# First layer of a four-layer graph network: a fixed TensorE order from the third column on, with one product ahead of the diagonal's sums

## The chip, the cores and the metric

One core of a Trainium2 chip. The metric is device time in microseconds (us); 25 timed runs of the kernel before in the last session have a median of 2253.3 us and lie between 2250.0 and 2257.1. Columns and blocks are counted from 0, so "column 2" is the third column.

## The reference, cut to what matters

Four layers pass `x` (4096 x 128) through a dense-stored 4096 x 4096 adjacency `adj`, each with a residual and a layer normalization. Only the first is changed:

```python
hw = h @ W
pos = (node_adj > 0).astype(hw.dtype)
...
h_plus = pos @ hw
e_plus = leaky_relu((h_plus @ a1 + h_minus @ a2)[:, 0], ALPHA)
scores = where(edge_adj > 0, e_plus[None, :], NEG_INF)      # cut
attn = softmax(scores, axis=1)
h_prime = attn * edge_adj @ hw
```

The score of an edge depends on its column alone. So, with weights `xe = exp(e)`, the softmax is a product of the adjacency with `xe * hw`, divided by a product of its mask with `xe`. The catch is that `e` of a column of 512 nodes needs the whole column of masks first.

## The kernel before

The adjacency is cut into 8 x 8 blocks of 512 x 512 (1 MB each). For column i the kernel reads block (i, j), VectorE makes the mask `pos`, TensorE adds up *edge sums* of the mask (short matmuls, four at a time in 32-column strips: four take 0.40 us in the trace, against 1.04 us for four over all 128 columns) and, for the blocks whose scores are already known (j < i), a *product* of the block with the scaled `hw` (four fp32 matmuls of 128 x 512, 3.4 us). When the edge sums of column i are whole, the scores of its nodes can be made:

```python
def scores(i, pe):
    parts <- pe                                   # VectorE or ScalarE
    sums = columns(parts)                         # TensorE: "score columns"
    e, den, leaky, clip on VectorE; exp on ScalarE
    nc.vector.tensor_mul(hw[:, tb, :], hw[:, tb, :], xe...)
    split3(xp[:, tb, :], 3, xe[:, tb])            # xp: three bf16 parts of xe
```

Only then can the blocks that waited for these scores be done: the diagonal's (i, i), and the two blocks above it that were kept in SBUF, (i-2, i) and (i-1, i), so that they are not read again. Their sums need `xp`, their products only `hw`. Blocks further above are read again in a *second sweep*. From column 3 on TensorE's order is pinned by `in_order`; the order of the other engines is the scheduler's.

```python
for i in range(3, NB):
    ...
    for g, group in enumerate(groups):            # two blocks a group
        got = [sums_of(i, j, ...) for j in group] # cut
        if g == 1:
            diagonal_sums(*rest)                  # needs xp
            for k in (i - 3, i - 2):
                above_sums(k, i - 1, kept[k, i - 1])
            diagonal_product(*rest)
        for n, (j, a, pos) in enumerate(got):
            if j < i:
                product(p, j, a, j == 0, False)
            if g == 0 and n == 0 and waiting:
                scores(i - 1, rest[2])
            if g == 1 and n < 2:
                above_product(i - 3 + n, i - 1, kept.pop(...))
```

TensorE's results go to PSUM, which this kernel divides into four pools of two banks: `ps_acc` (products), `ps_den` (edge sums), `ps_mm` (sums of kept blocks) and `ps_tr` (transposes and score columns). Blocks come into five rotating buffers.

## Time and profile before

| | before |
|---|---|
| median of the first three runs | 2254.38 us |
| span of the profiled run | 2250.1 us |
| TensorE busy | 95% |
| mean granted TensorE clock | 0.986 |
| first layer, to its last transposes | about 350 us |

In the timelines quoted below a line gives the start (us from the span's start), the length, engine, line of the source, operation, output<-inputs and shape, and in brackets the idle time before it with the instruction that ended it. `pden<-pos,xp` are the sums that wait for xp, `pacc<-chunk,hw` a product, `pacc<-keep,hw` a product of a kept block, `ptr<-sel,parts` the score columns. PE is TensorE, DVE VectorE, ACT ScalarE; L379 is line 379 of the kernel; `numT` is where the products of all columns are added up. A product's four fp32 matmuls show as x8 in these lines. A half-clock window is a stretch in which the trace shows a granted clock of 0.50, as from 82 to 88 us in before. The prediction shows the lines of before.

### The profile page before, as it was taken

To read this page: it belongs to the slowest core of one execution; us is meant where nothing else is said; L and a number is where in the kernel's file an instruction comes from. 1 tells how busy PE (TensorE), PEld (TensorE's weight loads), DVE (VectorE), ACT (ScalarE), POOL (GpSimd) and SP (SyncE) were. 2 spreads that over 40 slices of the span, in tenths; PEclk is the share of its full clock that TensorE was granted. 3 is DMA by queue.
4 is the path that set the end of the run, shared out by engine and by line. 5 is a ranking of instruction groups with operands and counts; after the bars stand their busy time and mean duration, and the time that the engine had idled before them with its cause. 6 is when DMAs were issued, how large, how long until landed. Compare 5 with 4: busy or idle time off the path is not lost. (4 is left out here: it accounts for less than half of the span.)

```text
span 2250.1 us, 22965 instructions
## 1 busy us (share of the span) xinstructions
PE 2140.8 (95%) x8633; PEld 847.8 (38%) x8636; DVE 1184.4 (53%) x1832; ACT 563.4 (25%) x1014; POOL 857.3 (38%) x539
## 2 busy tenths in 40 slices
PE   8899999999999999999999999978999899999997
PEld 3334354444444444444443333322222222233333
DVE  5544472000011100000025777789999999999995
ACT  6645110000000000000032322335333433332213
POOL 0000000000000000000004666688999899989990
PEclk9999999999999999999999999989999999999999
DMA  9776658888777676778766556614666566645544
GB/s 393 300 270 245 219 185 274 302 299 300 263 257 244 227 271 236 264 270 279 264 237 229 206 206 219 220 67 169 240 228 231 200 241 246 219 139 204 187 169 170
DMA packets 87145, 528.18 MB, mean 235 GB/s; under 512 B 9328, under 2 KB 15472, under 8 KB 25712
## 3 DMA queue, kind: packets, MB, share of 16 engines
q1 hardware_dynamic: 80288, 521.64, 65.7%
q10 hardware_dynamic: 6736, 4.98, 0.7%
q8 instruction: 70, 1.15, 0.2%
q14 instruction: 51, 0.42, 0.1%
HBM read 524.49 MB, written 2.10 MB: 234 GB/s over the span
## 5 line engine op out<-in xcount | busy, mean ns | idle before, releaser
L840 DVE SCALAR_TENSOR_TENSOR tau<-D,es,a 128x1024 f32<-128x1024 f32 (+1 forms) x640 | 649.5, 1071 | 52.5 <-ACT a L812 32.0
L848 POOL TENSOR_TENSOR tau<-tau,chunk 128x1024 f32<-128x1024 f32 x192 | 459.0, 2391 | 12.7 <-DVE tau L840 12.0
L746 POOL TENSOR_TENSOR x<-x,B2R 128x512 f32<-128x512 f32 x8 | 10.2, 1272 | 1169.3 <-PE px L137 1169.3
L864 PE MATMUL num<-tau,hc 128*32 128x512 f32 x2048 | 332.0, 615 | 12.3 <-POOL tau L848 5.8
L864 PE MATMUL den<-tau,cs 128*32 128x512 f32 x2048 | 336.4, 604 | 2.1 <-DVE tau L840 0.4
L951 PE MATMUL pp<-chunk,xT 128*128 128x512 f32 (+1 forms) x488 | 231.7, 604 | 0.0
L812 ACT ACTIVATE a<-chunk 128x1024 f32<-128x1024 f32 x160 | 164.3, 1027 | 249.7 <-DVE tau L846 191.4
L638 PE MATMUL pacc<-chunk,t 128*128 128x512 f32 x512 | 223.5, 592 | 0.0
L638 PE MATMUL pacc<-chunk,v 128*128 128x512 f32 x512 | 222.5, 592 | 0.0
L638 PE MATMUL pacc<-chunk,x 128*128 128x512 f32 x512 | 222.1, 592 | 0.0
L847 POOL TENSOR_TENSOR tau<-tau,chunk 128x320 f32<-128x320 f32 x192 | 167.7, 874 | 134.2 <-DVE tau L840 74.5
L1078 PE MATMUL pp<-chunk,w 128*128 128x512 f32 x448 | 203.6, 598 | 1.5 <-DVE oT L722 0.8
L379 PE MATMUL pacc<-chunk,hw 128*128 128x512 f32 x408 | 191.5, 614 | 2.7 <-DVE hw L421 1.4
L846 DVE TENSOR_TENSOR tau<-tau,a 128x704 f32<-128x704 f32 x186 | 165.7, 891 | 0.0
L854 POOL TENSOR_TENSOR tau<-tau,chunk 128x1024 f32<-128x1024 f32 x64 | 152.3, 2379 | 1.0
L864 PEld LDWEIGHTS num<-tau,hc 128*32 128x32 f32 x2048 | 61.3, 110 | 230.9 <-issue 126.2
L864 PEld LDWEIGHTS den<-tau,cs 128*32 128x32 f32 x2048 | 79.1, 111 | 175.0 <-issue 96.2
L638 PEld LDWEIGHTS pacc<-chunk,v 128*128 128x128 f32 x512 | 97.2, 190 | 122.0 <-issue 122.0
L638 PEld LDWEIGHTS pacc<-chunk,x 128*128 128x128 f32 x512 | 96.3, 190 | 115.8 <-issue 115.8
L638 PEld LDWEIGHTS pacc<-chunk,t 128*128 128x128 f32 x512 | 96.1, 190 | 115.3 <-issue 115.3
L951 PEld LDWEIGHTS pp<-chunk,xT 128*128 128x128 f32 x488 | 85.7, 190 | 128.6 <-issue 125.8
L685 DVE COPY w<-ptr 128x512 f32<-128x512 f32 x8 | 5.5, 692 | 241.5 <-PE ptr L137 241.5
(233 smaller groups left out, 1686.0 us busy)
## 6 DMA issues: line engine op xcount, KB each, us to landing
chunk<-in_adjT SPq DMA_DIRECT2D x386, 1024.0 KB, 4.8
chunk<-in_adj SPq DMA_DIRECT2D x80, 1024.0 KB, 4.9
chunk<-in_adj SPq DMA_DIRECT2D x32, 512.0 KB, 4.8
keep<-in_adjT SPq DMA_DIRECT2D x13, 1024.0 KB, 9.4
xT<-in_xT ACTq DMA_DIRECT2D x8, 256.0 KB, 6.6
out<-o ACTq DMA_DIRECT2D x7, 256.0 KB, 2.3
W1A<-in_w1a ACTq DMA_DIRECT2D x1, 384.0 KB, 5.6
W1B<-in_w1b ACTq DMA_DIRECT2D x1, 384.0 KB, 7.5
```

The lines of the kernel that those rows point to most:

```text
L379: in_order(nc.tensor.matmul(p, hw[:, j * TB + k, :], a[:, k, :], start=first and k == 0, stop=last and k == TB - 1))
L638: nc.tensor.matmul(p, stationary(c * TB + k), a[:, k, :], start=n == 0 and k == 0, stop=n == NB - 1 and k == TB - 1)
L746: nc.gpsimd.tensor_tensor(x[:, tb, :], x[:, tb, :], B2R[:, None, :].to_broadcast([P, TB, F]), ALU.add)
L812: nc.scalar.activation(ap, a, AF.Copy, accum_out=deg[:, nt, self.mp:self.mp + 1])
L840: nc.vector.scalar_tensor_tensor(flat(tau[:, q:q + n]), flat(self.D[:, q:q + n]), es[:, nt, head:head + 1], ap, op0=ALU.max, op1=ALU.mult)
L846: nc.vector.tensor_tensor(t2[:, 0:OWN], t[:, 0:OWN], (a if only else ap)[:, 0:OWN], ALU.mult)
L847: nc.gpsimd.tensor_tensor(t2[:, OWN:WB], t[:, OWN:WB], a[:, OWN:WB], ALU.mult)
L848: nc.gpsimd.tensor_tensor(t2[:, WB:2 * WB], t[:, WB:2 * WB], a, ALU.mult)
L854: nc.gpsimd.tensor_tensor(tau2[:, 2:4, :], tau[:, 2:4, :], rep(a, 2), ALU.mult)
L864: nc.tensor.matmul(acc[32 * q:32 * q + 32, :], weights(nt, head, is_den), r[:, q, :], start=nt == 0, stop=nt == NT - 1)
L951: nc.tensor.matmul(p, y[:, c * TB + k, :], a[:, k, lo:lo + n], start=c == blocks[0] and k == 0, stop=end)
L1078: nc.tensor.matmul(p, w[:, c * TB + k, :], a[:, k, :], start=c == 0 and k == 0, stop=c == NB - 1 and k == TB - 1)
```

## The change

Its intent: let TensorE have something to do while VectorE makes xp, keep a kept block's product from waiting for an accumulator's bank, and bring column 2 into the same fixed order. Cut to its core:

```diff
-            for i in range(3):
+            for i in range(2):
...
-                    if n == 2 and i == 2:
-                        above_sums(0, 1, kept[0, 1])
-                        above_product(0, 1, kept[0, 1])
...
+            for i in range(2, NB):
+                if i == 2:
+                    groups = [[5, 6], [], [7, 0], [3, 4], [1, 2]]
+                    owed = [(0, 1)]
...
+                        if i == 2 and first:
+                            keep_busy(lambda k: got[-1][2][:, k, :], TB)
...
+                products(sums(groups[0], True), 1)
+                second = sums(groups[1])
+                products(second[:1])
+                owed_sums()
+                diagonal_product(*rest)
+                if i > 2:
+                    above_product(*owed[0], kept[owed[0]], ps_tr, "ptr")
+                products(second[1:])
+                for n, group in enumerate(groups[2:], 3):
+                    got = sums(group)
+                    products(got)
+                    if n == len(groups):
+                        above_product(*owed[-1], kept[owed[-1]])
...
-                        rows[i] = ps_den.tile([P, IB], F32, name="pden"), None
+                        rows[i] = (ps_mm.tile(...) if i == 1 else ps_den.tile(...)), None
...
+                    if g == 4 and n == 1:
+                        diagonal_product(*rest)
+                        todo.append(NB - 1)
```

`keep_busy` issues dummy matmuls, whose results nobody reads. The last two pieces are in the second sweep: row 1's sums get a bank of another pool (so do the sums of one of the last two kept blocks, cut here), and column 7's diagonal product is put between two other products.

More of the change, by code (lines that the diff above doesn't have):

```diff
@@ L394, in add, with above_sums @@
                     nc.vector.tensor_add(blk, part, blk)
-            def above_sums(i, j, a):
-                pe = ps_mm.tile([P, IB], F32, name="pmm")
+            def above_sums(i, j, a, pool=ps_mm, name="pmm"):
+                pe = pool.tile([P, IB], F32, name=name)
                 edge_sums(pe, masks(a), j, xp, True, True)
@@ L401, in above_sums, with above_product @@
                 nc.vector.tensor_add(blk, pe, blk)
-            def above_product(i, j, a):
-                p = ps_acc.tile([P, IB], F32, name="pacc")
+            def above_product(i, j, a, pool=ps_acc, name="pacc"):
+                p = pool.tile([P, IB], F32, name=name)
                 product(p, j, a, True, True)
@@ L467, in layer0 @@
             ordered.append(None)
-            for i in range(3, NB):
-                first = [*range(i - 1), *range(i + 3, NB)]
-                pe = ps_den.tile([P, IB], F32, name="pden")
-                p = None
-                def sums_of(i, j, pe, first, last, pool=None, name="chunk"):
-                    a = chunk(pool or ld, adjT, i, j, name, True)
-                    pos = masks(a)
-                    edge_sums(pe, pos, j, both, first, last)
-                    count_bad(a, i * NB + j)
-                    return j, a, pos
-                last_sums = i == NB - 1
-                pairs = [*first, i - 1, i]
-                groups = [pairs[n:n + 2] for n in range(0, len(pairs), 2)]
-                for g, group in enumerate(groups):
-                    got = []
-                    for k, j in [*waiting[:1], *((None, j) for j in group), *waiting[1:]] if g == 0 else [(None, j) for j in group]:
-                        if k is not None:
-                            kept[k, j] = sums_of(k, j, rest[2], False, (k, j) == waiting[-1], l0k, f"keep{j - k}")[1]
-                        else:
-                            got.append(sums_of(i, j, pe, j == first[0], last_sums and j == i))
-                    if g == 1:
-                        diagonal_sums(*rest)
-                        for k in (i - 3, i - 2):
-                            above_sums(k, i - 1, kept[k, i - 1])
-                        diagonal_product(*rest)
-                    if g == 0:
-                        p = ps_acc.tile([P, IB], F32, name="pacc")
-                    for n, (j, a, pos) in enumerate(got):
@@ new lines, in sums_of, with keep, sums, products @@
+            def sums_of(i, j, pe, first, last, pool=ld, name="chunk"):
+                a = chunk(pool, adjT, i, j, name, True)
+                pos = masks(a)
+                edge_sums(pe, pos, j, both, first, last)
+                count_bad(a, i * NB + j)
+                return j, a, pos
+            def keep(i, j, pe, last):
+                kept[i, j] = sums_of(i, j, pe, False, last, l0k, f"keep{j - i}")[1]
+                return j, None, None
+            for i in range(2, NB):
+                pe = ps_den.tile([P, IB], F32, name="pden")
+                p = ps_acc.tile([P, IB], F32, name="pacc")
+                if i == 2:
+                    groups = [[5, 6], [], [7, 0], [3, 4], [1, 2]]
+                    owed = [(0, 1)]
+                else:
+                    order = [*range(i - 1), *range(i + 3, NB), i - 1, i]
+                    groups = [order[n:n + 2] for n in range(0, NB, 2) if order[n:n + 2]]
+                    owed = [(i - 3, i - 1), (i - 2, i - 1)]
+                def sums(group, first=False):
+                    got = []
+                    for n, j in enumerate(group):
+                        if first and n == 0 and waiting:
+                            keep(*waiting[0], rest[2], len(waiting) == 1)
+                        if i < j <= i + 2:
+                            keep(i, j, pe, False)
+                        else:
+                            got.append(sums_of(i, j, pe, first and n == 0, j == i and i in (2, NB - 1)))
+                        if i == 2 and first:
+                            keep_busy(lambda k: got[-1][2][:, k, :], TB)
+                    if first and len(waiting) == 2:
+                        keep(*waiting[1], rest[2], True)
+                    return got
+                def products(got, before=0):
+                    for n, (j, a, _) in enumerate(got):
@@ L499, in layer0, with owed_sums @@
                         if j < i:
                             product(p, j, a, j == 0, False)
-                        if g == 0 and n == 0 and waiting:
+                        if n == 0 and before and waiting:
                             scores(i - 1, rest[2])
-                        if g == 1 and n < 2:
-                            above_product(i - 3 + n, i - 1, kept.pop((i - 3 + n, i - 1)))
-                    if g == len(groups) - 1:
+                def owed_sums():
+                    diagonal_sums(*rest)
+                    for k, j in owed:
+                        above_sums(k, j, kept[k, j])
@@ L506, in layer0 @@
                         rest = (i, p, pe, got[-1][1], got[-1][2])
-                waiting = [(i, j) for j in range(i + 1, min(i + 3, NB))]
+                        if i == 2:
+                            scores(i, pe)
+                waiting = [(i, j) for j in range(i + 1, min(i + 3, NB))] if i > 2 else []
                 if i == 5:
@@ L553, in layer0 @@
                     if j == i + 3:
-                        rows[i] = ps_den.tile([P, IB], F32, name="pden"), None
+                        rows[i] = (ps_mm.tile([P, IB], F32, name="pmm") if i == 1 else ps_den.tile([P, IB], F32, name="pden")), None
                     edge_sums(rows[i][0], masks(a), j, xp, j == i + 3, j == NB - 1)
@@ L559, in layer0 @@
                 if g == 6:
-                    for k in (NB - 3, NB - 2):
-                        above_sums(k, NB - 1, kept[k, NB - 1])
-                for i, j, a in got:
+                    above_sums(NB - 3, NB - 1, kept[NB - 3, NB - 1])
+                    above_sums(NB - 2, NB - 1, kept[NB - 2, NB - 1], ps_den, "pden")
+                for n, (i, j, a) in enumerate(got):
+                    if g == 4 and n == 1:
+                        diagonal_product(*rest)
+                        todo.append(NB - 1)
                     if j == i + 3:
@@ L572, in layer0 @@
                         todo.append(i)
-                if g == 4:
-                    diagonal_product(*rest)
-                    todo.append(NB - 1)
                 if g in (6, 8):
```

## The prediction

> **What bounds the kernel now.** I first read the busy time by engine: TensorE is busy 95% of the 2250.1 us span and no other engine above 53%. A busy total says nothing of a change of order, so I then cut the span into stretches: from 360 to 1000 us TensorE is never idle, after 1000 us VectorE and GpSimd fill up, and the first layer, which is all that the change edits, ends near 344 us. The reordered list of each engine says the same: the last 6689 of 8393 rows on TensorE and all GpSimd work are in the order of before. So a gain must come out of the first layer's idle time and is then carried unchanged to the end.
>
> The chain that ended last does not reach back into this layer usefully; the waits of TensorE from 55 to 300 us do:
>
> ```profile
> engine line waited for: us in total, times, longest us
> PE pden L367 <- DVE xp L304: 9.0, 4, 2.3
> PE pden L367 <- DVE pos L310: 5.7, 3, 2.4
> PE pacc L379 <- ACT numT L389: 1.8, 1, 1.8
> PE pacc L379 <- DVE numT L407: 1.6, 2, 0.8
> PE pacc L379 <- DVE numT L394: 1.4, 1, 1.4
> PE ptr L374 <- DVE parts L414: 0.8, 1, 0.8
> PE pden L367 <- DVE xT L394: 0.8, 1, 0.8
> PE pacc L379 <- DVE hw L421: 0.6, 1, 0.6
> ```
>
> They sum to 21.7 us. Then the timeline of TensorE says where each lies. One turn of a column (the fourth) reads:
>
> ```profile
> 113.84 3.70 PE L379 MATMUL pacc<-chunk,hw 128*128 128x512 f32 x8
> 117.38 0.95 PE L374 MATMUL ptr<-sel,parts 128*128 128x2 f32 x8
> 118.19 3.68 PE L379 MATMUL pacc<-chunk,hw 128*128 128x512 f32 x8
> 121.80 0.61 PE L367 MATMUL pden<-pos,both 128*32 128x512 bf16 x8
> 124.64 0.40 PE L367 MATMUL pden<-pos,xp 128*32 128x512 bf16 x4 [2.23 <-DVE xp L304]
> ```
>
> The scores go out at 117.38, one product (x8 records, 3.4 us from start to start where another follows) and two groups of edge sums run beside VectorE's chain, and then the diagonal's sums need xp, which comes 7.2 us after 117.38. The same wait stands at 156.33 (2.23), 192.18 (2.35) and 229.69 (2.23). The worst place is the turn from the third to the fourth column:
>
> ```profile
> 78.84 1.05 PE L374 MATMUL ptr<-sel,parts 128*128 128x2 f32 x8 [0.80 <-DVE parts L414]
> 81.68 0.48 PE L367 MATMUL pden<-pos,both 128*32 128x512 bf16 x4 [1.78 <-DVE pos L310]
> 84.52 0.62 PE L367 MATMUL pden<-pos,both 128*32 128x512 bf16 x4 [2.36 <-DVE pos L310]
> 85.07 8.91 PE L379 MATMUL pacc<-chunk,hw 128*128 128x512 f32 x16
> ```
>
> Two products take 8.91 us here against 7.13 elsewhere. The stretches show why, and that the memory is the other limit up to here:
>
> ```profile
> 60.00:70.00 10.00, 10.00 (x37) 3.18 (x35) 5.31 (x8) 7.31 (x9) 0.00 (x0) 0.93 1.01 420
> ...
> 80.00:90.00 10.00, 5.96 (x16) 2.38 (x17) 8.80 (x17) 8.11 (x9) 0.00 (x0) 0.66 0.20 81
> ```
>
> The columns are TensorE, weight loads, VectorE, ScalarE, GpSimd, then granted clock, DMA share and GB/s. To about 73 us the transfers are saturated at 420 GB/s, one 1 MB block per 2.5 us; from 82 to 90 us nothing is loaded, as all five buffers wait for late products.
>
> [...] cut into single microseconds the clock is exactly 0.50 or 1.00 but for the boundaries, half from about 58.0 to 61.3, 82 to 88.7 and 157 to 160.2. [...] 2.23 us of idle before 156.33 was followed by a half-clock window. [...] So a wait for xp also stops the products behind it that are ready; the change's whole lever is program order. [...] a product must have a bank whose reader is done; the 0.78 us waits at 105.06 and 136.75 are that.
>
> **The change, part by part.**
>
> 1. One product ahead of the diagonal. From column 4 on (counting from 0) the second group's first product moves before the xp sums. TensorE then has 0.8 (score columns) + 3.4 + 0.55 + 3.4 = 8.2 us from the start of the score columns, against 7.2 for xp. Four waits go: 2.23 + 2.23 + 2.35 + 2.23 = 9.0 us. The half clock after the second goes too: 8.70 - 7.13 = 1.6.
> 2. A kept block's product in the transposes' banks. Removes 0.78 twice, and with the diagonal's product no longer just behind a two-bank queue the 1.76 wait for ScalarE's copy: 3.3 us.
> 3. The third column in fixed order. Same 4 products, none added. Now the product of (2,1) and the kept (0,1) are last before the score columns, so the copy of the sums (0.8) hides; and VectorE's list now has both masks of column 3's first blocks ahead of the score chain, so 1.78 and 2.36 go, and the half clock (8.91 - 7.13 = 1.8): 6.7 us. What it costs: these two products cannot start before the last block of column 2. Counting blocks of 2.5 us in order of issue, with block (2,5) down by 54.3 at the latest (ScalarE reads it then), block (2,2), seven later, lands about 71.8, its mask is done at 73.0; edge sums 0.3, two products 6.9: score columns at 80.3, not 78.8. So +1.5, net 5.2 us.
> 4. Eight added dummy matmuls in the third column, 1.04 us per four by the rows of their kind: 2.1 us, all in idle time before 61 us (1.59 + 0.64 of waits stand there now, and half clock to 61.3). They cost nothing [...]; but the diagonal's product, which now fills this gap, goes behind xp. That start is neither gain nor loss within 1 us, and the DMA sets the pace there anyway.
> 5. The second sweep: row 1's sums get another bank and the last diagonal's product goes between two products, so 0.80 (sums) and 1.37 (VectorE's add into numT) go: 2.2 us.
>
> Sum: 9.0 + 1.6 + 3.3 + 5.2 + 2.2 = 21.3 us. Work is otherwise equal: the same products, sums and transfers. Checked by column: score columns start now at 78.8, 117.4, 149.1, 184.8, 222.4, 264.3; I expect about 80, 110, 138, 172, 207, 247.
>
> **The rivals.**
>
> A. New waits take part of it back. TensorE is busy with real work nearly throughout, so transfers must follow: five buffers, each freed by a product. For: loading averages 240 GB/s from 78 to 113 us but comes in bursts at full rate, and at the end of column 2 TensorE will idle some 2 us for the last two blocks, which may fetch a half-clock window (1.7 us). Further, xp's margin in part 1 is 1 us, and in the last column VectorE has three masks before the chain and ScalarE a count of 2.1 us before the copy of the sums. Each is 0 to 2 us; I take 3 us off.
>
> B. The column turns are memory bound and the waits only move: a mask waiting for its block replaces xp. Against: from 80 to 90 us the DMA share is 0.20, and from 100 to 260 between 0.48 and 1.04, mostly under 0.85. The time would then be near 2248.
>
> C. The gain is lost later, as a later stage waits for something that doesn't move. Against: TensorE is at 10.00 of every 10 us from 360 on and those loads come by the same five buffers. The tail with GpSimd starts from products that all shift. The time would be unchanged, 2254.
>
> D. The clock repays more than counted, [...] and starts of sweeps also shrink: 25 us, 2229.
>
> **Range and chances.** 21.3 less 3 is 18 us, so 2254.4 - 18.4 = 2236. The three times of before spread over 5 us, so I add 2 to 3 us each side for the runs to the doubt of A and D: 2229 to 2246. 2% is 45 us; twice the whole idle time that I can name would be wanted. Faster by over 2%: 0.01. Slower by over 2%: 0.01, only if a fixed order deadlocks itself with the loads for long. Within 2%: 0.98.
>
> **What would show it.** Right: no wait of TensorE for xp after 100 us; none for numT by lines of kept products; clock 1.00 from 90 to 260 us; score columns at the times above, the second sweep's end some 18 us earlier, and equal lengths after it. Step 3 is wrong if TensorE still waits over 1 us for masks between 80 and 90, or if the score columns of column 2 come after 83. Part 1 is wrong if xp comes later than 8.2 us after its score columns. The prediction falls if waits for masks that wait for blocks sum to over 8 us, or if the stretch from 360 to the end changes by over 4 us.

## The result, and the profile after

| | before | after |
|---|---|---|
| median (4 runs each, same rounds) | 2253.66 us | 2230.57 us |
| lowest to highest | 2251.02 to 2255.97 | 2229.57 to 2231.09 |
| span of the profiled run | 2250.1 | 2227.8 |

The ratio is 0.9897, with a 95% interval from 0.988 to 0.9915. It is the mean time of the changed kernel's fast runs over that of the fast runs of before in the same rounds, so not quite the ratio of the medians. The change is 23.1 us faster, 1.0%: inside the predicted range, within 2%, and 5.4 us better than the predicted 2236.

The waits of TensorE between 55 and 300 us, after, in full (waiter, what it waited for: us in total, times, longest):

```profile
PE pden L367 <- DVE pos L310: 4.0, 3, 1.6
PE pacc L379 <- DVE numT L407: 1.1, 2, 0.9
```

Eight groups with 21.7 us have become two with 5.1. There is no wait for xp left. The turn of column 4, in the timeline of TensorE, now reads:

```profile
108.21 0.95 PE L374 MATMUL ptr<-sel,parts 128*128 128x2 f32 x8
109.02 3.68 PE L379 MATMUL pacc<-chunk,hw 128*128 128x512 f32 x8
112.63 0.62 PE L367 MATMUL pden<-pos,both 128*32 128x512 bf16 x8
113.17 3.70 PE L379 MATMUL pacc<-chunk,hw 128*128 128x512 f32 x8
116.80 0.40 PE L367 MATMUL pden<-pos,xp 128*32 128x512 bf16 x4
117.03 0.60 PE L367 MATMUL pmm<-pos,xp 128*32 128x512 bf16 x8
117.57 3.70 PE L379 MATMUL pacc<-chunk,hw 128*128 128x512 f32 x8
121.10 3.60 PE L379 MATMUL ptr<-keep,hw 128*128 128x512 f32 x8
```

The second product (113.17) stands where TensorE was idle for 2.23 us, the xp sums follow 8.59 us after the score columns without a bracket, and the kept block's product (121.10) goes to `ptr` straight behind the diagonal's. VectorE's last part of xp was ready 7.43 us after the score columns.

The turn from column 2 to 3:

```profile
75.48 3.60 PE L379 MATMUL pacc<-keep,hw 128*128 128x512 f32 x8
78.92 0.95 PE L374 MATMUL ptr<-sel,parts 128*128 128x2 f32 x8
79.80 0.62 PE L367 MATMUL pden<-pos,both 128*32 128x512 bf16 x8
80.34 7.13 PE L379 MATMUL pacc<-chunk,hw 128*128 128x512 f32 x16
```

No gap, and the two products take 7.13 us, not 8.91. The stretches (columns as in the prediction: five engines, clock, DMA share, GB/s):

```profile
80.00:90.00 10.00, 10.00 (x48) 4.09 (x41) 8.37 (x18) 6.53 (x9) 0.00 (x0) 1.00 0.69 251
360.00:1000.00 640.00, 640.00 (x1621) 292.35 (x1620) 42.41 (x60) 32.25 (x50) 0.00 (x0) 1.00 0.78 267
```

TensorE is busy all of 80 to 90 us (5.96 of 10 before), its clock is full (1.00 against 0.66), and the loads run on (251 GB/s against 81). From 360 to 1000 us TensorE is busy for all 640.00 us in both kernels.

To compare kernels I use one length from each trace: from the score columns of column 1 to the first transpose of `x` after the second layer's first product, which I call the **seam** (344.72 us before, 324.36 after). It drops the jitter of the start (column 1's score columns come at 53.95 to 55.73 us over the 14 traces). It is 290.10 us before and 269.75 after: 20.4 us gained. The rest, from the seam to the end, is 1905.4 before and 1903.4 after.

| from column 1's score columns to | before | after | gained in this stretch |
|---|---|---|---|
| column 2's | 24.22 | 24.31 | -0.1 |
| column 3's | 62.76 | 53.60 | 9.2 |
| column 4's | 94.45 | 82.14 | 3.2 |
| column 5's | 130.18 | 115.46 | 2.4 |
| column 6's | 167.81 | 152.18 | 0.9 |
| column 7's | 209.72 | 191.99 | 2.1 |
| the seam | 290.10 | 269.75 | 2.6 |

### The profile page after: what moved, and what is told of

It reads as the page before. It is cut to its first block, busy times and chain, and to the rows that moved or that the text cites.

```text
span 2227.8 us, 22992 instructions
## 1 busy us (share of the span) xinstructions
PE 2135.1 (96%) x8644; PEld 847.9 (38%) x8644; DVE 1184.2 (53%) x1832; ACT 562.5 (25%) x1014; POOL 857.6 (38%) x539
## 3 DMA queue, kind: packets, MB, share of 16 engines
q8 instruction: 70, 1.15, 0.2%
## 5 line engine op out<-in xcount | busy, mean ns | idle before, releaser
L874 POOL TENSOR_TENSOR tau<-tau,chunk 128x1024 f32<-128x1024 f32 x192 | 459.4, 2392 | 12.3 <-DVE tau L866 11.7
```

Source lines behind the costliest of these rows:

```text
L874: nc.gpsimd.tensor_tensor(t2[:, WB:2 * WB], t[:, WB:2 * WB], a, ALU.mult)
```

## The experiments

Each kernel with timing was run in several rounds beside the kernel before. "Length" is the one just defined.

| run | median us | lowest to highest | length us | rest after the seam |
|---|---|---|---|---|
| before, two traces | 2253.3 | 2250.0 to 2257.1 (25 runs) | 290.10, 290.03 | 1905.4, 1905.4 |
| after, two traces | 2230.57, 2230.36 | 2229.6 to 2231.1 (8 runs) | 269.75, 268.97 | 1903.4, 1904.1 |
| e1, after without the product ahead | 2235.95 | 2232.7 to 2243.1 | 273.29 | 1903.4 |
| e2, after with the old bank | 2235.44 | 2234.4 to 2238.1 | 277.72 | 1904.4 |
| e3, after with column 2 free | 2239.36 | 2237.4 to 2244.1 | 276.82 | 1907.3 |
| e4, after without dummies | 2229.10 | 2228.4 to 2230.9 | 269.61 | 1904.8 |
| e5, after with the old sweep | 2234.47 | 2232.1 to 2237.5 | 273.38 | 1905.3 |
| e6, before with the product ahead | 2246.77 | 2242.8 to 2249.8 | 282.32 | 1906.1 |
| e7, e1 with its gaps filled | 2238.24 | 2236.9 to 2239.1 | 277.67 | 1903.5 |
| e8, before with the new bank | 2248.84 | 2246.2 to 2253.5 (19 runs) | 286.72 | 1905.9 |
| e9, before with both | 2240.23 | 2237.2 to 2244.2 | 277.75 | 1907.0 |
| v4, three more steps on after | 2228.84 | 2228.2 to 2231.1 | 267.83 | 1903.1 |

All gave correct results. e1 to e4 ran in a session without the changed kernel, so they are compared with its medians from two other sessions; the kernel before's medians in the four sessions lie between 2253.3 and 2254.0.

A length still holds a scatter of column 2, where the clock is at half for 3.4 us in most traces, for 6.8 us in some and in e6 not at all (its half products there take 1.98 us each; the first of e8's takes 3.78). Its stretch takes 22.7 us in e6, 24.2 in both traces of before and 25.6 in e8, which all have the same code there; with the changed code it takes 24.3 to 24.8, but 25.3 to 25.4 in e2 and e5. So differences of lengths up to 1.5 us can be column 2's alone.

### e1: without the product ahead

```diff
                 second = sums(groups[1])
-                products(second[:1])
                 owed_sums()
...
-                products(second[1:])
+                products(second)
```

> The changed kernel, but the second group's first product goes behind the diagonal's again. Theory (TensorE in order, xp comes 7.2 us after the score columns start): the wait for xp comes back at columns 4 to 7, 2.2 to 2.4 us each, 9 us, and perhaps one half-clock window (1.7), so 8 to 11 us slower than the changed kernel's 2230.6: 2239 to 2242. Rival (loads set the pace, each part is worth less than its waits): under 4 us slower, and waits for masks shrink by what xp takes.

Measured: 5.4 to 5.6 us slower than the changed kernel's two sessions in the medians, 3.5 to 4.3 in length. Two full waits for xp are back, at columns 4 and 6 (2.45 us each); at column 5 there is none and at column 7 one of 0.22. So the theory's "four waits" was wrong, and the rival's size is nearer in the trace, but not for its reason: no wait for a load took over. The trace of e1 shows what decides. Column 4 (TensorE, then VectorE's list from the same chain):

```profile
107.80 0.95 PE L374 MATMUL ptr<-sel,parts 128*128 128x2 f32 x8
...
115.28 0.40 PE L367 MATMUL pden<-pos,xp 128*32 128x512 bf16 x4 [2.45 <-DVE xp L304]
```

```profile
110.30 1.22 DVE L310 TENSOR_SCALAR pos<-chunk 128x2048 bf16<-128x2048 f32 x1
111.44 0.16 DVE L306 TENSOR_TENSOR xe<-xe,xp 128x4 f32<-128x4 f32 x1
111.51 1.22 DVE L310 TENSOR_SCALAR pos<-keep 128x2048 bf16<-128x2048 f32 x1
112.64 0.17 DVE L304 CAST xp<-xe 128x4 bf16<-128x4 f32 x1
```

Between the tiny steps of the xp chain (0.16 and 0.17 us) the scheduler has put masks of 1.22 us, four in this column, and xp is ready 7.43 us after the score columns. In column 5 of the same run there is no mask inside:

```profile
141.10 0.17 DVE L304 CAST xp<-xe 128x4 bf16<-128x4 f32 x1
141.30 0.17 DVE L306 TENSOR_TENSOR xe<-xe,xp 128x4 f32<-128x4 f32 x1
141.50 0.18 DVE L304 CAST xp<-xe 128x4 bf16<-128x4 f32 x1
```

xp is ready after 3.42 us, and TensorE, which gets there after 4.86, doesn't wait. The kernel before had four masks inside the chain in each of columns 4 to 7 (7.2 to 7.3 us). So the wait for xp was half VectorE's order. The change moved that too, though its diff doesn't name VectorE: the changed kernel has 4, 2, 4 and 0 masks inside, for xp after 7.43, 5.20, 7.43 and 3.43 us.

### e2: the kept product in the accumulators' banks again

```diff
-                    above_product(*owed[0], kept[owed[0]], ps_tr, "ptr")
+                    above_product(*owed[0], kept[owed[0]])
```

> The changed kernel, but the kept block's product behind the diagonal's goes to the accumulators' two banks again. My prediction's list counted 3.3 us for the banks (0.78 twice and 1.76). Theory now: in the new order this product comes straight behind the diagonal's, one bank is the column's own and the other the diagonal's, so it waits for ScalarE's copy in each of columns 3 to 7, about 1 to 1.8 us each: 5 to 9 us slower than the changed kernel. Rival (the list): 3 us slower, with waits in columns 3 and 4 only.

Measured: 4.9 to 5.1 us slower in the medians, 8.0 to 8.8 in length, of which 1.0 lies in column 2, which the edit doesn't touch (the traced run is one of the two slowest). There are four waits for ScalarE's copy of the diagonal's product, in columns 3 to 6: 0.68 three times and one of 2.91. That one, TensorE and then ScalarE:

```profile
125.07 5.40 PE L379 MATMUL pacc<-keep,hw 128*128 128x512 f32 x8 [2.91 <-ACT numT L389]
```

```profile
122.54 1.91 ACT L351 ACTIVATE junk<-keep 128x2048 fp8e4<-128x2048 f32 x1 [0.50 <-DMA keep<-in_adjT]
124.36 0.19 ACT L351 ACTIVATION_READ_ACCUMULATOR junk<-keep 128x1 f32 x1
124.45 0.56 ACT L389 COPY numT<-pacc 128x512 f32<-128x512 f32 x1
```

The product that frees the bank was over near 122.1. But in ScalarE's list a count of another block stands before the copy; this count waited for its block's load until 122.54 and took 1.91 us, and the copy came behind it. The product that waited then ran at half clock for part of its way (5.40 us instead of 3.60; the mean clock from 115 to 145 us is 0.94). The theory holds in kind, with smaller waits but for that one; the rival ("columns 3 and 4 only, 3 us") falls.

### e3: column 2 left to the scheduler

```diff
-            for i in range(2):
+            for i in range(3):
...
+                    if n == 2 and i == 2:
+                        above_sums(0, 1, kept[0, 1])
+                        above_product(0, 1, kept[0, 1])
...
-            for i in range(2, NB):
+            for i in range(3, NB):
```

> The changed kernel with the third column left to the scheduler as before (no dummies there, no fixed order until column 3). Theory: the waits of 1.78 and 2.36 us for masks and the half-clock window at the turn to column 3 come back, 6 us, 5 to 8 us slower than the changed kernel. Rival (up to there the loads set the pace, so what is lost there is caught up in column 3 while blocks wait in the buffers): under 3 us slower.

Measured: 8.8 to 9.0 us slower in the medians, a little above the theory's range, and 7.1 to 7.9 in length, within it. The waits at the turn to column 3 are back (0.80, 1.78 and 2.44 us), half clock from about 82.5 to 89.3 us too (two products take 9.39 us, and the mean clock from 78 to 115 us is 0.91), and the stretch from column 2's to column 3's score columns is 37.3 us, against 29.3. Columns 3 to 7 don't catch any of it up.

### e4: without the dummy matmuls of column 2

```diff
-                        if i == 2 and first:
-                            keep_busy(lambda k: got[-1][2][:, k, :], TB)
```

> The changed kernel without the eight dummy matmuls in the third column. Theory: they stand in idle time, and in the changed trace the half-clock window (59.7 to 62.6 us) falls on the second four of them; without them the window comes earlier or reaches further, onto the diagonal's product, and the loads set the pace of this column anyway: 0 to 1 us slower. Rival [...]: a half-clock window over a product, 1.7 us or more slower. Second rival (they only delay the xp sums): up to 1 us faster.

Measured: 1.3 to 1.5 us faster in the medians, with overlapping runs (2228.4 to 2230.9 against 2229.6 to 2231.1), and a length of 269.61, between the two of the changed kernel: no difference that I would claim. The timeline of TensorE shows one on the way:

```profile
60.02 0.62 PE L367 MATMUL pden<-pos,both 128*32 128x512 bf16 x4 [2.26 <-DVE pos L310]
61.31 0.62 PE L367 MATMUL pden<-pos,xp 128*32 128x512 bf16 x4 [0.68 <-DVE xp L304]
61.72 0.64 PE L367 MATMUL pmm<-pos,xp 128*32 128x512 bf16 x4
62.29 5.86 PE L379 MATMUL pacc<-chunk,hw 128*128 128x512 f32 x8
```

Here the clock is at 0.50 from about 59.8 to 66.7 us and the diagonal's product takes 5.86 us in place of 3.70; in the changed kernel's first trace it is at 0.50 from about 59.4 to 62.8 (the expectation read this a little short), mostly over dummies. Column 2's score columns come 1.1 us later, column 3's stretch is 0.4 us shorter, and column 6's shorter by the 0.93 us wait that only the first trace of the changed kernel has. But this isn't shown to be the dummies' work: e2 and e5 have the same dummies, are at half clock for as long (about 57.7 to 64.5 us by the lengths of their matmuls), their diagonal's product takes 4.63 and 4.67 us, and their score columns come 1.0 us later. That the dummies ever hold off half clock is not shown; in the total they are worth nothing.

### e5: the second sweep as before

```diff
-                        rows[i] = (ps_mm.tile(...) if i == 1 else ps_den.tile(...)), None
+                        rows[i] = ps_den.tile([P, IB], F32, name="pden"), None
...
-                    if g == 4 and n == 1:
-                        diagonal_product(*rest)
-                        todo.append(NB - 1)
...
+                if g == 4:
+                    diagonal_product(*rest)
+                    todo.append(NB - 1)
```

(and the sums of the two last kept blocks both in `ps_mm` again)

> The changed kernel with the second sweep as before. Theory: the two waits for VectorE's adds (0.80 and 1.37 us) come back and nothing behind them catches up, as TensorE is then never idle: 2.2 to 2.6 us slower than the changed kernel in the same rounds. Rival (the loads set where the sweep ends): no difference.

Measured: 4.1 us slower in the medians. From column 7's score columns to the seam e5 takes 80.33 us, before 80.38 and the changed kernel 77.76: 2.6 us, as the theory says. The other 1.1 us by which its length exceeds the changed kernel's first are not of this edit: 0.6 lies before column 3's score columns (column 2's longer half clock) and 0.4 in the waits of columns 5 and 6 (1.41 and 1.11 us, against 1.15 and 0.93). The waits that are back are the two of before:

```profile
260.23 0.62 PE L367 MATMUL pden<-pos,xp 128*32 128x512 bf16 x8 [0.80 <-DVE xT L394]
265.81 3.70 PE L379 MATMUL pacc<-chunk,hw 128*128 128x512 f32 x8 [1.33 <-DVE numT L394]
```

### e6, e8, e9: the product ahead, the bank, and both, on the kernel before

e6:

```diff
                     if g == 1:
+                        if got[0][0] < i:
+                            product(p, got[0][0], got[0][1], got[0][0] == 0, False)
                         diagonal_sums(*rest)
...
-                        if j < i:
+                        if j < i and not (g == 1 and n == 0):
```

> The kernel before with nothing changed but the one product ahead of the diagonal. My prediction said that this alone removes four waits for xp, 9.0 us, and a half-clock window, 1.6. Undoing it in the changed kernel cost only 3 us in the trace, because VectorE's list had fewer masks inside the xp chain there. Theory: in the kernel before VectorE's list still has three to four masks inside, xp comes 6 to 7.2 us after the score columns, and hiding it is worth 6 to 10 us: 2244 to 2248. Rival (loads take most of it, as blocks come no sooner): under 4 us, 2250 or more.

e8 (e9 is e6 and e8 together):

```diff
-                            above_product(i - 3 + n, i - 1, kept.pop(...))
+                            above_product(i - 3 + n, i - 1, kept.pop(...), *((ps_acc, "pacc") if n else (ps_tr, "ptr")))
```

> The kernel before with nothing changed but the first kept block's product in the transposes' banks. Theory: it removes 0.78 twice and 1.76, and the waits for xp stay, so 1.5 to 3.5 us faster than before; with the product ahead alone (7.5 us in the trace) that makes some 10. Rival: nothing, as the wait moves to the second kept product.

> The kernel before with both: the product ahead and the kept product in the transposes' banks; third column and second sweep as before. Theory (the product ahead puts the kept product straight behind the diagonal's, 0.7 to 1.9 us of wait for ScalarE's copy in columns 3 to 6, which only the bank removes): more than the sum of the two alone, 11 to 14 us faster than before, 2240 to 2243. Rival (they add): the sum.

Measured in medians of the same rounds: e6 is 7.2 us faster than before, e8 4.5, e9 13.1. In length: 7.8, 3.4 and 12.3, or 6.3, 4.7 and 12.4 behind column 2's score columns, where the edits begin. The theories of e6 and e9 hold. e8's holds in kind, as the three waits for a bank are gone and those for xp stay, but 4.5 is above its 1.5 to 3.5; in its trace 1.65 us are column 5's, where the half clock of before is missing. e6 shows its mechanism plainly: xp comes as late as before (7.2 to 7.4 us after the score columns, four masks inside) and no longer matters, as TensorE gets there at 8.6. But some of the gain turns into the new wait that e9's theory names:

```profile
99.42 3.70 PE L379 MATMUL pacc<-keep,hw 128*128 128x512 f32 x8 [1.86 <-ACT numT L389]
130.32 3.70 PE L379 MATMUL pacc<-keep,hw 128*128 128x512 f32 x8 [1.03 <-ACT numT L389]
160.86 3.70 PE L379 MATMUL pacc<-keep,hw 128*128 128x512 f32 x8 [0.67 <-ACT numT L389]
```

In the kernel before another product stood between the diagonal's and the kept one in columns 4 to 7; moved ahead, it no longer gives ScalarE the time to empty the bank. With 0.68 in column 6 these waits are 4.2 us, of which 1.76 were there before. In e9 they are gone. That the two together beat their sum (13.1 against 11.7, 12.3 against 11.2) fits, but the difference is within the scatter of single traces and of e6's and e9's runs, so it isn't shown.

### e7: the gaps of e1 filled with dummies

e1's six runs, in the order of their clock: 

| mean granted clock | time us |
|---|---|
| 0.989 | 2232.68 |
| 0.988 | 2234.22, 2233.95 |
| 0.986 | 2237.68 |
| 0.984 | 2243.09, 2242.71 |

```diff
                 second = sums(groups[1])
-                products(second[:1])
+                if i > 2:
+                    keep_busy(lambda k: second[0][2][:, k % TB, :], 2 * TB)
                 owed_sums()
```

> The run without the product ahead, with eight dummy matmuls (1.8 us) put into the wait for xp of each column from 3 on. The wait itself stays. That run scattered from 2232.7 to 2243.1 us, its mean clock falling from 0.989 to 0.984 as the time rose, while the changed kernel scatters by 1.5 us. Theory (an idle gap of 2.2 to 2.5 us sometimes falls so that a half-clock window follows it, over products): filled, the scatter shrinks to some 2 us, all clocks are 0.988 or more and the median falls to 2233 or 2234. Rival (the scatter has another source, the loads for one): scatter and median stay, 2236.

Measured: 2236.9 to 2239.1 us, clocks 0.987 to 0.989. The scatter fell from 10.4 to 2.2 us, as the theory says; the session was another than e1's, but the kernel before scatters by 7 us in both. The median did not fall (2238.24 against 2235.95), since I had put dummies into five columns of which only two have a full wait to fill; elsewhere they are work on the path (2.0 us in column 3 and 1.5 in column 7, against e1's trace). The theory holds for the scatter and misses on the median and, by 0.001, on the clocks.

### Second traces of both kernels

> The changed kernel again. Score columns of the first layer at the same times as in its first trace within 1 us; the stretch after the first layer, 1903.4 us there and 1905.4 in the trace of before, shows what this stretch scatters by itself: theory 1903 to 1907 whatever the kernel, so that the 2 us are no effect of the change.

> A second trace of the kernel before. The same waits for xp in columns 4 to 7, 2.2 to 2.4 us each; half-clock windows behind some of them, not the same ones as in the first trace (there only behind column 5's), if where they fall is chance.

The changed kernel's second trace has the score columns at the same distances within 0.8 us and no wait of 0.93 us in column 6; the 1.15 us wait in column 5 is in both. The trace of before repeats within 0.1 us, with the half-clock window behind column 5's wait in the same place (0.50 from 157 to 160 us), so there the expectation that it falls elsewhere was wrong: in these two traces it doesn't. (e8 has the same four waits, at other times, and half clock behind none.) The rest after the seam lies between 1903.1 and 1907.3 us over all 14 traces, and not without order: the five on the kernel before have 1905.4 to 1907.0, eight of the nine on the changed kernel 1903.1 to 1905.3. But it goes with the clock. The four shortest rests (v4, after, e1 and e7, 1903.1 to 1903.5) are of traces with a mean granted clock of 0.988 or 0.989; of the ten others only the second of after (1904.1) and e5 (1905.3) have 0.988, the rest 0.985 to 0.987. In the first pair, one minus the clock, summed over pieces of 1 us from the seam to the end, makes 22.6 us before and 20.9 after: 1.6 of the 1.9 us between them. As e5, made from the changed kernel, is with before, I put the 2 us of the first pair down to the time at half clock, and not to the edit.

### v4: three more steps

```diff
-                        above_product(*owed[-1], kept[owed[-1]])
+                        above_product(*owed[-1], kept[owed[-1]], ps_tr, "ptr")
...
-                if i == 5:
+                if i == 7:
                     tc.keep_in_program_order(nc.sync.dma_start(x, ...))
...
-                products(sums(groups[0], True), 1)
+                if i == 2:
+                    sums([5], True)
+                    diagonal_product(*rest)
+                    sums([6])
+                else:
+                    products(sums(groups[0], True), 1)
```

(the diagonal's product is then left out behind `owed_sums()` in column 2)

> Three further steps on the changed kernel: the last kept product of a column also goes to the transposes' banks (so the next column's products don't wait for VectorE's add, 0.2 and 0.93 us in the trace), the 2 MB load of x moves from column 5 to column 7 (the 1.15 us wait for a mask in column 5, whose block lands late while that load runs), and in the third column the diagonal's product, which needs no xp, goes ahead of the sums (its score columns 3 us earlier). Theory (the waits add up): 3 to 5 us faster than the changed kernel. Rival (the loads set the pace of columns 5 and 6, as in the run without dummies, which lost 1.3 us in column 2 and had it back by column 6): under 1.5 us faster.

Measured: 2228.84 us, 1.5 faster than the changed kernel in the same rounds, with one run of four above it; the length is 1.1 to 1.9 us shorter. The theory's 3 to 5 are missed, and the rival's size is right. The waits of columns 5 and 6 are gone and column 5's stretch falls from 33.3 to 32.0 us. The third step is the miss: column 2's score columns come only 0.6 to 0.7 us earlier, and this stands in their place (timeline of TensorE):

```profile
67.26 0.40 PE L367 MATMUL pden<-pos,both 128*32 128x512 bf16 x4 [1.71 <-DVE pos L310]
105.51 0.40 PE L367 MATMUL pden<-pos,both 128*32 128x512 bf16 x4 [1.16 <-DVE pos L310]
```

In column 2 TensorE waits 1.71 us for a mask that VectorE makes from 65.99 to 67.21 us, straight behind its add into `xT`, which had waited 2.03 us for TensorE's sums. The DMA is saturated in column 2 (share 1.01 and 421 GB/s from 54 to 73 us, in the first traces of both kernels), but a wait for a load isn't shown here, so the rival's reason, "the loads set the pace", isn't either. Column 3 has a wait of 1.16 us for a mask that neither trace of the changed kernel has there. v4 is the fastest kernel, by a margin near the scatter.

## Why the prediction was right

**Where the gain sits: right.** The score columns of columns 2 to 7 were expected at 80, 110, 138, 172, 207 and 247 us and came at 78.9, 108.2, 136.8, 170.1, 206.8 and 246.6. The stretch from 360 to 1000 us is as busy as before (640.00 of 640.00 us). The rest after the seam is 1.3 to 2.0 us shorter in the two pairs of traces, which goes with the time at half clock (in the first pair 22.6 us lost before and 20.9 after).

**Part 1, one product ahead: right that the waits go, mis-sized alone.** "Four waits go ... 9.0 us" and the half clock's 1.6: no wait for xp is left, and TensorE reaches it after 8.6 us (predicted 8.2). But 10.6 us is not what the step is worth. On the kernel before it gave 7.2 in the medians (e6), since the step creates waits for a bank, up to 1.03 us in columns 4 to 6 and 2.5 us in all, that the prediction gave to neither part. Undone in the changed kernel it cost 3.5 to 4.3 in length (e1), since VectorE's list has fewer masks inside the xp chain there. I had taken "7.2 us for xp" for a property of the chain; it is 3.4 us of chain and the rest the scheduler's masks.

**Part 2, the banks: right in kind.** In e8 the three waits of the 3.3 us are gone; columns 3 and 4, where they stood, are 3.1 us shorter. In the new order the bank holds off more: 4.9 to 5.1 us in e2's medians. Its trace has 8.0, with 1.8 for the half clock behind the longest wait and 1.0 in column 2.

**Part 3, column 2: right, with one wrong step and a slip.** The waits of 1.78 and 2.36 us and the half-clock window went, and e3 gives them back. The step that failed is "score columns at 80.3, not 78.8" (its terms add up to 80.2): they came at 78.92. I had counted blocks of 2.5 us from the time at which ScalarE read block (2,5), the latest that it can have landed; block (2,2)'s mask began at 70.33 us, after a short wait for its load, not at 71.8. And the 0.8 us that I added as hidden lie before 78.8, so they were in the 1.5 already. The net should have read 4.4 by my own numbers, and the sum 20.5. From column 2's to column 3's score columns 9.2 us went, against 8.5 in the named waits of that stretch.

**Part 4, the dummies: right that they are worth nothing at the end.** Half clock came all the same, mostly over dummies in the changed kernel's first trace (0.50 from about 59.4 to 62.8 us), but into the diagonal's product in e2 and e5 (4.63 and 4.67 us, against 3.70).

**Part 5, the second sweep: 2.2 predicted, 2.6 measured,** in the changed kernel and again in e5.

**The sum.** 21.3 us was predicted before rivals; the lengths give 20.4 and 21.1 in the two pairs of traces. **Rival A** took 3 us off that. New waits did come (1.15 us in column 5 in both traces, 0.93 in column 6 in one, 0.2 in column 3), some 1.4 to 2.3 us, but what I had underestimated (1.4 us in column 2, 0.7 in column 3, 0.4 in the sweep) made up for them and for the slip of 0.8: that the sum came out so near is partly luck. So the point of 2236 was too slow by the haircut. The rest of the 5.4 us lies partly behind the seam, as above, and partly in **rival D**, which I named and gave no weight in the point: the fastest run of before and the fastest of after are 20.5 us apart (2250.0 and 2229.6), but the medians 23, because the runs of before lie up to 7 us above their fastest, at clocks from 0.988 down to 0.983 or 0.984, and the changed kernel's within 1.5. That idle gaps are what opens this scatter is shown for e1, whose runs lie 10.4 us apart with two gaps of 2.45 us and 2.2 us apart with the gaps filled (e7); for the kernel before it is an inference from the same gaps and a similar spread. Such gaps are not the only source: e5's runs lie 5.4 us apart, at clocks of 0.987 and 0.988, and its trace has no wait above 1.6 us. **Rivals B and C** fell: e3 and e5 show nothing caught up, and the stretch from 360 to 1000 us is unchanged. In column 2 the DMA was saturated (share 1.01 from 54 to 73 us); that the loads set TensorE's pace there is not shown.

## What to carry to other kernels

On an engine that works in program order, as TensorE did here (2.23 us idle in front of a product that e6 could move ahead), look at what stands in front of a late wait and put independent work of at least its length there; then look at once at what the moved work had been hiding, here the emptying of a bank: 2.5 us of new waits in e6, gone in e9. Before counting a latency as fixed, read the list of the engine that makes the result: half of this one was other work of 1.2 us put between steps of 0.2 us. Putting VectorE's list in order might then have done in place of the product ahead, as in e1's column 5, where no mask stands inside the chain and TensorE doesn't wait; no run tried that alone. And take the spread of the runs into the estimate: with gaps of 2 us closed it went from 7 us to 1.5 here, and the medians lie further apart than the fastest runs (23 against 20.5 us).

## What the traces show of the clock and of the lists

- Half clock followed a gap of 2.23 us in both traces of before: they show clock 0.50 for some 3.4 us right behind column 5's wait for xp, and the two products there take 8.70 and 8.79 us. In the first of before half clock begins near 57.96, 81.86 and 156.96 us and lasts 3.4 or 6.8 us (the prediction's ends of 61.3 and 160.2 are read a little short); column 5's gap lies from 154.10 to 156.33. Behind the other three waits for xp in each of these traces (2.23 to 2.35 us) and behind all four in e8 (2.22 to 2.45 us) two products take 7.13 us, and e1, with two gaps of 2.45 us, has a clock of 1.00 in each stretch from 78 to 340 us. So in these traces it was not a gap's length alone that decided; what else did is not shown.
- Gaps in the middle went with scatter between runs of one kernel: up to 10.4 us of 2235 in e1 (0.5%, more than any single edit here moved a median), and 2.2 us with them filled (e7).
- Whether dummy matmuls can take half clock on themselves isn't settled here: the product behind them took 3.70 us in both traces of the changed kernel, 4.63 and 4.67 in e2 and e5 with the same dummies, and 5.86 without (e4).
- The order of VectorE's and ScalarE's lists, a scheduler's choice, decided how late a short chain ended: 3.4 us with no mask inside, 7.2 to 7.4 with four. ScalarE's copy of a bank came 2.3 us after the product's end, behind one count of 1.91 us (e2).
